# Three narrow router products: from stationary activations to stationary weights on three column groups, issued in steps

## The chip, the cores and the metric

The kernel runs on one core of a Trainium2 chip. The metric is the device time in microseconds of one execution. It was run three times; the median is the number to be changed. One further execution was recorded by the hardware profiler, and all times "by the profile" are from that one, counted from the start of its span.

## The reference

The reference is one forward pass of a graph network on 512 tokens of 768 features, in four blocks. Each block adds a graph layer and an attention layer to x, and then a feed-forward layer. The feed-forward layers of blocks 0, 2 and 3 are mixtures of experts; each begins with a router, which is a product of the normalized tokens with a very narrow matrix. Cut to the routers (in the case's names):

```python
# block 0: 8 experts of 192, two per token, weights from sqrt(softplus)
scores  = jnp.sqrt(jax.nn.softplus(flat @ gate_w))            # [512,768] @ [768,8]
_, indices = jax.lax.top_k(scores + gate_bias, 2)
weights = take_along_axis(scores, indices, axis=1); weights /= clip(weights.sum(1), 1e-06)
# block 2: a shared expert and 3 routed ones, two per token
routing_probs = jax.nn.sigmoid(x @ router_w + routing_bias)   # [512,768] @ [768,3]
scores, indices = jax.lax.top_k(routing_probs, 2); scores /= scores.sum(-1)
# block 3: 8 experts, one per token, at most 64 tokens each
router_probs = jax.nn.softmax(xf @ router_w)                  # [512,768] @ [768,8]
expert_gate, expert_index = max(router_probs), argmax(router_probs)
```

All is in float32.

## The kernel before

Tokens lie token-major, as 4 tiles of 128 tokens (`NT`), or feature-major, as 6 chunks of 128 features by 512 tokens (`KC`; `xfT` is the normalized input of a feed-forward layer in this form). `normed` makes both: layernorm on VectorE (DVE), transposes on TensorE (PE, L246), copies out of PSUM in turn by ScalarE (ACT, L202) and DVE (L204). It returns the second half of the transposes as a function `rest`, which the next product calls after its first four parts.

Nearly all large products are one level of Strassen's scheme. `strassen_feature` (products at L461, feature-major result) works in three chunks of seven products, each of three 128x256 matmuls; `strassen_add` (L553) adds its results into x. The sums of the left operand are made by DVE (L392 to L394), those of the weights by GpSimd (POOL, `SplitB`, L411 to L414) ahead of time from weights that the SP queue has loaded. `staged` delays the second half of each chunk behind the first half of the next one, also across calls. A float32 matmul stands in the profile as two records, each with its own weight load ("PEld"); they are called passes here. So the 24 matmuls of a router are 48 passes.

After each of these products the kernel calls `tick`, which takes one step of the first generator in the list `background`; side work is so put between products of the main stream. `delayed(9, step)` waits nine ticks and then does all of its step at once. The written order is only the start: instructions of different streams are then placed on each engine by a scheduler, and the order on each engine is fixed before the run; each engine works through its own in order.

`router` (L338) loads the narrow weights `rt_w` (768 by `e`, with `e` 8 or 3) and, for each token tile, runs six matmuls in which the 128x128 piece of `xfT` is stationary and the `e` columns of the weights are moving (L345). Its result is [token, expert] in PSUM. It is used in three places:

- Block 0, `weights_by_expert`: ten ticks into the first `strassen_feature` of `up_part(0)`, the router and all that follows run in one piece: copy of the logits to `lg` (L954), softplus by Abs, Exp and Ln on ACT with small DVE operations between, Sqrt, `ranks` (a comparison of all pairs of experts, L330 to L335), normalization, four transposes of the weights `sc` (L985), a copy and a write to DRAM (`c_dram`, L988), from which `load_weights` reads rows spread over partitions into `pc` (L1000). `pc` multiplies the hidden values in `multiplied` (L1019, POOL).
- Block 2, `route`: called between the first two `strassen_feature` of the shared expert; logits plus bias in `pr` (L1565), Sigmoid, `ranks`, normalization. It is first used by the down product of the first routed expert.
- Block 3: right after `normed`, with no other product beside it; the maximum of the logits (L1656), Exp, `ranks`, positions by small matmuls (L1676), and then dispatch, experts and output. This is the end of the kernel.

`row_tile` gives row buffers from a pool of two, which the bias rows (`row`, L168) use as well; `psum` gives one of eight PSUM banks.

Of the kernel before, what the change touches and what calls it, by code (L numbers as in the profile page):

```python
# [97 lines left out]
def kernel(ctx: ExitStack, tc: tile.TileContext, a: dict, out: bass.AP):  # L98
# [27 lines left out]
    def psum():  # L126
        return psp.tile([P, 512], FP, tag="ps", name="ps")
# [35 lines left out]
    def row_tile(name, n=D):  # L163
        return rowp.tile([P, KC * (P + 2)], FP, tag="row", name=name)[:, :n]
# [170 lines left out]
        V.tensor_reduce(r, gt, AX.X, ALU.add)  # L335
        return r

    def router(xT, w_dram, e):  # L338

        w = small.tile([P, KC, e], FP, tag="rt_w", name="rt_w", bufs=2)  # L340
        nc.sync.dma_start(w, w_dram.rearrange("(k p) e -> p k e", p=P))
        ps = psum()[:, : NT * e].rearrange("p (t e) -> p t e", t=NT)
        for t in range(NT):
            for k in range(KC):
                T.matmul(ps[:, t, :], xT[:, k, ts(t, P)], w[:, k, :], start=k == 0, stop=k == KC - 1)  # L345
        return ps

# [75 lines left out]
    def drain():  # L425
        while background:
            tick()

    def delayed(n, step):

        for _ in range(n):
            yield
        step()

    held = []

# [510 lines left out]
    _, xfT, xs, rest = normed(x, "xf", 1e-5)  # L947
    with tc.tile_pool(name="ffn0", bufs=2) as fp:
        E = 8
        def weights_by_expert():  # L950
            gb = tiny(E, name="gb")
            nc.sync.dma_start(gb, spread(a["L0_ffn_gate_bias"], 0, E))
            lg = tiny(NT, E, name="lg")
            V.tensor_copy(lg, router(xfT, a["L0_ffn_gate_w"], E))  # L954

            ex, u, big, sm = (tiny(NT, E, name=n) for n in ("sp_e", "sp_u", "sp_b", "sp_s"))
            S.activation(ex, lg, AF.Abs)
            S.activation(ex, ex, AF.Exp, scale=-1.0)
            V.tensor_scalar(u, ex, 1.0, None, op0=ALU.add)
            S.activation(big, u, AF.Ln)  # L960
            V.tensor_scalar(sm, ex, -1.0 / 3.0, 0.5, op0=ALU.mult, op1=ALU.add)
            V.tensor_mul(sm, sm, ex)
            V.tensor_scalar(sm, sm, -1.0, 1.0, op0=ALU.mult, op1=ALU.add)
            V.tensor_mul(sm, sm, ex)
            V.tensor_scalar(u, ex, 0.01, None, op0=ALU.is_lt)
            V.tensor_sub(sm, sm, big)
            V.tensor_mul(sm, sm, u)
            V.tensor_add(big, big, sm)
            V.tensor_scalar(lg, lg, 0.0, None, op0=ALU.max)
            V.tensor_add(lg, lg, big)  # L970
            sc = tiny(NT, E, name="sc")
            S.activation(sc, lg, AF.Sqrt)
            V.tensor_add(lg, sc, gb[:, None, :].to_broadcast([P, NT, E]))
            sel = ranks(lg, E)
            V.tensor_scalar(sel, sel, 2.0, None, op0=ALU.is_lt)
            V.tensor_mul(sc, sc, sel)
            tot = tiny(NT, name="tot")
            V.tensor_reduce(tot, sc, AX.X, ALU.add)
            V.tensor_scalar(tot, tot, 1e-6, None, op0=ALU.max)
            V.reciprocal(tot, tot)  # L980
            for t in range(NT):
                V.tensor_scalar(sc[:, t, :], sc[:, t, :], tot[:, t : t + 1], None, op0=ALU.mult)
            ps = psum()
            for t in range(NT):
                T.transpose(ps[:E, ts(t, P)], sc[:, t, :], ident)  # L985
            scT = row_tile("scT", N)[:E]
            V.tensor_copy(scT, ps[:E])
            nc.sync.dma_start(c_dram, scT)  # L988


        c_dram = tc.dram_tile([E, N], FP, name="c_dram")
        pc = fp.tile([P, KC, N], FP, name="pc", bufs=1)

        def load_weights(g):
            for f in range(KC):
                p = 0
                while p < P:
                    at = g * D + f * P + p
                    n = min(P - p, 192 - at % 192)
                    nc.sync.dma_start(pc[p : p + n, f, :],  # L1000
                                      c_dram[at // 192 : at // 192 + 1, :].to_broadcast([n, N]))
                    p += n

        def up_part(g):

            hid = feature_major("hid")
            sums = SplitA(hid, G, False)

            def gated(c, i, j, ps):
                h = hid[:, 3 * j + c, ts(i, HT)]  # L1010
                V.tensor_scalar(h, ps, 10.0, None, op0=ALU.min)
                S.activation(h, h, AF.Silu)

            def multiplied(c, i, j, ps):
                f = 3 * j + c
                h = hid[:, f, ts(i, HT)]
                V.tensor_scalar(ps, ps, -10.0, 10.0, op0=ALU.max, op1=ALU.min)
                V.tensor_mul(h, h, ps)
                G.tensor_mul(h, h, pc[:, f, ts(i, HT)])  # L1019

            if g == 0:
                background.append(delayed(9, weights_by_expert))
            strassen_feature(xs, ready(a["L0_ffn_w1"][:, ts(g, D)]) if g else nexts.pop(), gated, None,
                             None if g else rest)
            yield
            load_weights(g)
            strassen_feature(xs, ready(a["L0_ffn_w3"][:, ts(g, D)]), multiplied,
                             sums.sums)
            flush()
            yield sums  # L1030

        pending = None
        for g in range(2):
            stages = up_part(g)
            next(stages)
            if pending:
                strassen_add(pending[1], ready(a["L0_ffn_w2"][ts(pending[0], D), :]), add_part)
            pending = g, next(stages)

        sw = w_tile()  # L1040
        wi = sw[:, : KC * 384].rearrange("p (k n) -> p k n", k=KC)
        for i, n in enumerate(("w1s", "w3s")):
            src = a[f"L0_ffn_{n}"].rearrange("(k p) n -> p k n", p=P)
            nc.sync.dma_start(wi[:, :, ts(i, P)], src[:, :, :P])
            nc.sync.dma_start(wi[:, :, 2 * P + i * HD : 2 * P + (i + 1) * HD], src[:, :, P:])
        w2a, w2b = sw[:, KC * 384 : KC * 384 + D], sw[:HD, KC * 384 + D : KC * 384 + 2 * D]
        nc.sync.dma_start(w2a, a["L0_ffn_w2s"][:P, :])
        nc.sync.dma_start(w2b, a["L0_ffn_w2s"][P:, :])
        last = ready(a["L0_ffn_w2"][D:, :])
        gat_w1 = ready(a["L1_gnn_W1"])  # L1050
        hid = feature_major("hid")

        def glu(dst, pg, pu):
            V.tensor_scalar(dst, pg, 10.0, None, op0=ALU.min)
            S.activation(dst, dst, AF.Silu)
            V.tensor_scalar(pu, pu, -10.0, 10.0, op0=ALU.max, op1=ALU.min)
            V.tensor_mul(dst, dst, pu)

        pg, pu = feature_product(wi, xfT, 0), feature_product(wi, xfT, P)
        glu(hid[:, 0, :], pg, pu)  # L1060
        ps = feature_product(wi, xfT, 2 * P)
        glu(hid[:HD, 1, :], ps[:HD], ps[HD:])
        strassen_add(pending[1], last, add_part)
        flush()
        token_product([hid[:, 0, :], hid[:HD, 1, :]], lambda k: (w2a, w2b)[k], add_to_x)
# [492 lines left out]
    with tc.tile_pool(name="ffn2", bufs=2) as fp:  # L1558
        E = 3
        pr = tiny(NT, E, name="pr")  # L1560

        def route():
            rb = tiny(E, name="rb")
            nc.sync.dma_start(rb, spread(a["L2_ffn_routing_bias"], 0, E))
            V.tensor_add(pr, router(xfT, a["L2_ffn_router_w"], E), rb[:, None, :].to_broadcast([P, NT, E]))  # L1565
            S.activation(pr, pr, AF.Sigmoid)
            sel = ranks(pr, E)
            V.tensor_scalar(sel, sel, 2.0, None, op0=ALU.is_lt)
            V.tensor_mul(pr, pr, sel)
            tot = tiny(NT, name="tot")  # L1570
            V.tensor_reduce(tot, pr, AX.X, ALU.add)
            V.reciprocal(tot, tot)
            V.tensor_mul(pr, pr, tot[:, :, None].to_broadcast([P, NT, E]))
# [43 lines left out]
        for e in range(E + 1):  # L1617
            for g in range(2):
                stages = up_part(e, g)
                next(stages)  # L1620
                if pending:
                    down_part(*pending)
                else:
                    route()
                pending = e, g, next(stages)
        down_part(*pending)
        flush()
# [23 lines left out]
    with tc.tile_pool(name="ffn3", bufs=1) as fp:  # L1651
        E, CAP = 8, N // 8
        lg = tiny(NT, E, name="lg")
        mx = tiny(NT, name="mx")
        ps = router(xfT, a["L3_ffn_router_w"], E)
        V.tensor_reduce(mx, ps, AX.X, ALU.max)  # L1656
        V.tensor_sub(lg, ps, mx[:, :, None].to_broadcast([P, NT, E]))
        S.activation(lg, lg, AF.Exp)
        V.tensor_reduce(mx, lg, AX.X, ALU.add)
        V.reciprocal(mx, mx)  # L1660
# [169 lines left out]
```

## Time and profile before

| what | value |
|---|---|
| median of 3 runs (lowest to highest) | 3228.47 us (3226.35 to 3235.73) |
| the profiled execution: its time, its span | 3229.27 us, 3227.6 us |
| PE, weight loads, DVE, ACT, POOL: busy share | 96%, 64%, 47%, 20%, 45% |
| mean granted TensorE clock | 0.981 |
| chain that ended last: PE, DVE, POOL | 81%, 9%, 4% |
| matmuls of the Strassen products on that chain (L461, L553) | 39%, 22% |
| router matmuls (L345) | 144 passes, median 256 ns each, overlapping |

A record of a matmul covers its own latency as well, and the next one starts before it ends; so the distance between starts is what a pass costs, and it is read from stretches: 12 passes of 128x256 in 2.75 us. "PEclk" is the clock that TensorE was granted, 1.00 at full speed. A bracket at the end of a line is idle time of the engine just before it, and what ended it. A busy PE need not be a fast one: the clock has to be read beside it.

### The profile page before, as it was taken

How to read it: one execution, taken by the hardware profiler on the slowest of the kernel's cores; microseconds unless marked ns; L12 is line 12 of the kernel's file. 1: busy time of each engine (PE TensorE's matmuls, PEld its weight loads, DVE VectorE, ACT ScalarE, POOL GpSimd, SP SyncE). 2: the span in 40 equal slices, each digit the busy share in tenths (PEclk: the TensorE clock that was granted, in tenths of full speed). 3: DMA queues.
4: the chain of work that ended last, by engine and by line, in shares of the span. 5: the costliest groups of instructions: out<-in, count | busy, mean ns of one | idle time of the engine just before them, and what ended most of it. 6: DMA issues, size and time to landing. Idle time of an engine off the chain costs nothing.

```text
span 3227.6 us, 32219 instructions
## 1 busy us (share of the span) xinstructions
PE 3094.6 (96%) x12097; PEld 2066.8 (64%) x12097; DVE 1524.1 (47%) x3433; ACT 637.7 (20%) x1268; POOL 1461.4 (45%) x1560
## 2 busy tenths in 40 slices
PE   8999999999999999999998999999999999999999
PEld 3445555555765776765684357777777775677755
DVE  7574444445446324446676535433333336453241
ACT  0132222222252110201441212100000001121101
POOL 0344444445225564464534254355555557355520
PEclk9999999999999999999999999999999999999999
DMA  3021221112202122321111422122222222131221
GB/s 111 14 79 69 69 69 69 69 69 108 88 30 93 59 101 76 108 94 68 45 67 68 119 82 98 59 88 88 89 88 88 89 86 84 70 108 59 89 97 59
DMA packets 92837, 255.23 MB, mean 79 GB/s; under 512 B 9905, under 2 KB 14897, under 8 KB 91530
## 3 DMA queue, kind: packets, MB, share of 16 engines
q1 hardware_dynamic: 92682, 253.18, 22.7%
q8 instruction: 95, 1.56, 0.2%
q14 instruction: 60, 0.49, 0.0%
HBM read 244.23 MB, written 8.93 MB: 78 GB/s over the span
## 4 chain that ended last, share of the span: by engine, by line
PE 81%; DVE 9%; POOL 4%; issue 3%; ACT 1%; DMA 0%; SPq 0%; POOLq 0%; DVEq 0%; ACTq 0%
PE ps L461 39%; PE ps L553 22%; PE ps L751 4%; PE ps L614 3%; PE ps L302 3%; DVE st_u L664 2%; PE ps L922 1%; PE ps L909 1%; PE ps L246 1%; DVE edge_w L637 1%; DVE edge_w L639 1%; POOL tw L411 1%; POOL w L412 1%; POOL tw L413 1%; PE ps L1711 1%
## 5 line engine op out<-in xcount | busy, mean ns | idle before, releaser
L411 POOL TENSOR_TENSOR tw<-w 128x384 f32<-128x384 f32 x246 | 249.9, 1025 | 1094.0 <-PE ps L461 324.0
L461 PE MATMUL ps<-sx,tw 128*128 128x256 f32 x1188 | 304.8, 381 | 3.3 <-DVE sx L393 2.3
L461 PE MATMUL ps<-sx,w 128*128 128x256 f32 x1188 | 293.2, 383 | 0.8 <-DVE room L1264 0.8
L553 PE MATMUL ps<-tw,sx 128*128 128x384 f32 x720 | 252.3, 489 | 9.6 <-POOL tw L413 5.8
L412 POOL TENSOR_TENSOR w<-w 128x384 f32<-128x384 f32 x246 | 253.0, 1036 | 8.5
L413 POOL TENSOR_TENSOR tw<-w 128x384 f32<-128x384 f32 x246 | 252.4, 1033 | 9.5
L414 POOL TENSOR_TENSOR tw<-w,tw 128x384 f32<-128x384 f32 x246 | 250.3, 1024 | 9.9
L553 PE MATMUL ps<-w,sx 128*128 128x384 f32 x720 | 252.5, 486 | 0.0
L461 PEld LDWEIGHTS ps<-sx,w 128*128 128x128 f32 x1188 | 227.4, 192 | 34.5 <-DVE room L1264 1.5
L461 PEld LDWEIGHTS ps<-sx,tw 128*128 128x128 f32 x1188 | 226.4, 191 | 35.4 <-PE ps L461 3.4
L553 PEld LDWEIGHTS ps<-tw,sx 128*128 128x128 f32 x720 | 136.1, 190 | 106.5 <-POOL sx L383 8.0
L583 DVE TENSOR_TENSOR x<-x,ps 128x384 f32<-128x384 f32 x218 | 116.1, 552 | 185.9 <-PE ps L553 185.7
L553 PEld LDWEIGHTS ps<-w,sx 128*128 128x128 f32 x720 | 136.8, 190 | 92.8
L504 DVE TENSOR_TENSOR st_u<-st_p,ps 128x256 f32<-128x256 f32 (+1 forms) x127 | 57.1, 450 | 271.9 <-PE ps L461 271.9
L477 ACT COPY st_p<-ps 128x256 f32<-128x256 f32 (+1 forms) x127 | 50.2, 395 | 667.5 <-PE ps L461 665.6
L461 PE MATMUL ps<-xfT,w 128*128 128x256 f32 x720 | 180.2, 389 | 0.1
L461 PE MATMUL ps<-tw,sx 128*128 128x384 f32 x456 | 166.7, 499 | 14.0 <-DVE st_u L499 6.0
L751 PE MATMUL ps<-edge_wT,h 128*128 128x512 f32 x384 | 168.0, 594 | 8.7 <-DVE edge_wT L204 8.7
L499 DVE TENSOR_TENSOR st_u<-st_p,ps 128x256 f32<-128x256 f32 (+1 forms) x127 | 57.1, 450 | 246.8 <-PE ps L461 143.0
L461 PE MATMUL ps<-w,sx 128*128 128x384 f32 x456 | 160.5, 489 | 1.0 <-DVE ps L505 1.0
L461 PEld LDWEIGHTS ps<-xfT,w 128*128 128x128 f32 x720 | 140.2, 195 | 24.2 <-ACT st_p L477 0.3
L553 PE MATMUL ps<-w,hid 128*128 128x384 f32 x432 | 143.1, 487 | 0.0
(460 smaller groups left out, 5093.3 us busy)
## 6 DMA issues: line engine op xcount, KB each, us to landing
w<-in_L_gnn_W SPq DMA_DIRECT2D x60, 768.0 KB, 6.2
w<-in_L_mix_fc_w SPq DMA_DIRECT2D x48, 768.0 KB, 6.9
row<-in_rows SPq DMA_DIRECT2D x39, 384.0 KB, 3.6
w<-in_L_mix_qkv_w SPq DMA_DIRECT2D x18, 768.0 KB, 7.3
w<-in_L_ffn_w SPq DMA_DIRECT2D x18, 768.0 KB, 6.7
w<-in_L_ffn_routed_gate SPq DMA_DIRECT2D x18, 768.0 KB, 6.0
w<-in_L_ffn_routed_up SPq DMA_DIRECT2D x18, 768.0 KB, 5.9
w<-in_L_ffn_routed_down SPq DMA_DIRECT2D x18, 768.0 KB, 6.0
```

The costliest lines, as they stand in the source:

```text
L302: T.matmul(ps, parts[k][:, ts(t, P)], w_of(k)[:, ts(c, HC)], start=k == 0, stop=k == n - 1)
L411: G.tensor_sub(tt[:, 0, k], b22[:, k], b12[:, k])
L412: G.tensor_sub(b12[:, k], b12[:, k], b11[:, k])
L413: G.tensor_sub(tt[:, 1, k], b22[:, k], b12[:, k])
L414: G.tensor_sub(tt[:, 2, k], b21[:, k], tt[:, 1, k])
L461: T.matmul(bank, l, r, start=start and k == 0, stop=stop and k == KC // 2 - 1, skip_group_check=True)
L499: V.tensor_add(b["u2"], b["p1r"], b["y"])
L553: T.matmul(b[name], l[:, k, ts(m, P)], r[:, k, :], start=start and k == 0, stop=k == KC // 2 - 1, skip_group_check=True)
L583: V.tensor_add(x[:, t, ts(j, HC)], x[:, t, ts(j, HC)], ps)
L614: T.matmul(acc[t], oh[:, 1, ts(t, P)], oh[:, 0, :], start=j == 0, stop=j == EC - 1)
L664: V.scalar_tensor_tensor(junk, h[:, t, :], 1.0, r, op0=ALU.mult, op1=ALU.mult, accum_out=sc[:, t : t + 1])
L751: T.matmul(ps, h[:, s, ts(f, P)], wT[:, s, :], start=s == 0, stop=s == NT - 1)
```

## The change

The router's operands change roles. The weights are padded with zeros to 32 columns per feature chunk (`rt_w` is now [128, 6, 32], one buffer, cleared by POOL and then loaded) and are stationary; `xfT` is moving, 512 tokens at a time. Three feature chunks go to three column groups of 32, which write partitions 0 to 31, 32 to 63 and 64 to 95 of one PSUM bank; two rounds of three add up all six chunks. The 96x512 result is copied to SBUF by ACT, and four small matmuls, with 128 tokens of it stationary and a constant `three` (three unit matrices below each other) moving, turn it to [token, expert] and add the three groups. The function is a generator, with steps between the product, the small matmuls and what follows. In block 0 it now starts at the fifth tick instead of the tenth and its chain is cut into pieces by `yield`; `drain()` finishes it before `load_weights`. In block 2 `route` is put into `background` too, and runs beside the second `strassen_feature`. In block 3 it is run through at once.

```diff
-    def router(xT, w_dram, e):
-        w = small.tile([P, KC, e], FP, tag="rt_w", name="rt_w", bufs=2)
-        nc.sync.dma_start(w, w_dram.rearrange("(k p) e -> p k e", p=P))
+    G3 = 3 * 32
+    three = const.tile([P, 8], FP, name="three")
+    V.tensor_add(three, ident[:, 0:8], ident[:, 32:40])
+    V.tensor_add(three, three, ident[:, 64:72])
+    def router_weights(w_dram, e):
+        w = small.tile([P, KC, 32], FP, tag="rt_w", name="rt_w", bufs=1)
+        G.memset(w, 0.0)
+        nc.sync.dma_start(w[:, :, :e], w_dram.rearrange("(k p) e -> p k e", p=P))
+        return w
+    def routed(w, xT, e, use):
+        ps = psum()
+        for r in range(KC // 3):
+            for g in range(3):
+                k = 3 * r + g
+                T.matmul(ps[ts(g, 32)], w[:, k, :], xT[:, k, :], start=r == 0, stop=r == KC // 3 - 1,
+                         skip_group_check=True)
+        part = row_tile("rt_p", N)
+        S.copy(part[:G3], ps[:G3])
+        yield
+        yield
         ps = psum()[:, : NT * e].rearrange("p (t e) -> p t e", t=NT)
         for t in range(NT):
-            for k in range(KC):
-                T.matmul(ps[:, t, :], xT[:, k, ts(t, P)], w[:, k, :], start=k == 0, stop=k == KC - 1)
-        return ps
+            T.matmul(ps[:, t, :], part[:G3, ts(t, P)], three[:G3, :e], start=True, stop=True)
+        use(ps)
...
-    def delayed(n, step):
+    def delayed(n, steps):
         for _ in range(n):
             yield
-        step()
+        yield from steps
...
+        rw = router_weights(a["L0_ffn_gate_w"], E)
         def weights_by_expert():
...
-            V.tensor_copy(lg, router(xfT, a["L0_ffn_gate_w"], E))
+            yield from routed(rw, xfT, E, lambda ps: V.tensor_copy(lg, ps))
             S.activation(ex, lg, AF.Abs)
             S.activation(ex, ex, AF.Exp, scale=-1.0)
+            yield
...
             V.tensor_scalar(u, ex, 0.01, None, op0=ALU.is_lt)
+            yield
...
             S.activation(sc, lg, AF.Sqrt)
+            yield
+            yield
...
+            for _ in range(4):
+                yield
             ps = psum()
             for t in range(NT):
                 T.transpose(ps[:E, ts(t, P)], sc[:, t, :], ident)
...
-                background.append(delayed(9, weights_by_expert))
+                background.append(delayed(4, weights_by_expert()))
...
             yield
+            if g == 0:
+                drain()
             load_weights(g)
...
         def route():
-            V.tensor_add(pr, router(xfT, a["L2_ffn_router_w"], E), rb[:, None, :].to_broadcast([P, NT, E]))
+            yield from routed(rw, xfT, E, lambda ps: V.tensor_add(
+                pr, ps, rb[:, None, :].to_broadcast([P, NT, E])))
             S.activation(pr, pr, AF.Sigmoid)
+            yield
+            yield
...
-                    route()
+                    background.append(route())
...
-        ps = router(xfT, a["L3_ffn_router_w"], E)
-        V.tensor_reduce(mx, ps, AX.X, ALU.max)
-        V.tensor_sub(lg, ps, mx[:, :, None].to_broadcast([P, NT, E]))
+        def scores(ps):
+            V.tensor_reduce(mx, ps, AX.X, ALU.max)
+            V.tensor_sub(lg, ps, mx[:, :, None].to_broadcast([P, NT, E]))
+        for _ in routed(router_weights(a["L3_ffn_router_w"], E), xfT, E, scores):
+            pass
```

On the engines, the order differs from before only around the three places. In block 0, PE now has: two matmuls of the product A22·T4, the first router matmul, one more of A22·T4, the other five router matmuls, three of A22·T4 for the next chunk, three on `sx`, the four small matmuls; the four transposes of `sc` follow 27 matmuls later (the first of them one matmul ahead of the other three). In block 2, the six router matmuls stand together after the first product of the second `strassen_feature`, and the small ones six matmuls later. In block 3, they follow the 24 transposes of `normed`.

## The prediction

> **What bounds the kernel now.** The page first: PE is 96% busy and holds 81% of the chain that ended last, so a saving counts only where PE works for nothing, works slowly, or waits. Then the timeline around the three router places, the granted clock by stretches, and the rows of narrow matmuls elsewhere. Block 0 and block 2:
>
> ```profile
> 1281.43 2.75 PE L461 MATMUL ps<-sx,tw 128*128 128x256 f32 x12
> 1284.02 7.40 PE L345 MATMUL ps<-rt_w,xfT 128*128 128x8 f32 x48
> 1291.27 2.05 PE L461 MATMUL ps<-sx,w 128*128 128x256 f32 x4
> 1293.12 2.77 PE L461 MATMUL ps<-sx,tw 128*128 128x256 f32 x6
> 1303.76 1.02 PE L985 MATMUL ps<-ident,sc 128*8 128x128 f32 x4 [7.02 <-DVE sc L982]
> ...
> 2068.47 6.84 PE L345 MATMUL ps<-rt_w,xfT 128*128 128x3 f32 x48
> 2075.18 2.91 PE L461 MATMUL ps<-xfT,w 128*128 128x256 f32 x6
> ```
>
> A Strassen pass costs (2.75 - 0.17)/12 = 0.215 us, a router pass 7.40/48 = 0.154 or 6.84/48 = 0.143. After the router, six passes take 2.8 to 2.9 instead of 1.46, and PE then waits 7.02 for the weights' chain. The clock, for block 0, 2 and 3 (columns: stretch, its length, PE busy, clock, DMA share, GB/s):
>
> ```profile
> 1283.80:1291.20 7.40, 7.40 (x50) 0.73 0.01 2
> 1291.20:1308.50 17.30, 10.28 (x30) 0.62 0.15 31
> 1308.50:1330.00 21.50, 21.50 (x101) 1.00 0.62 181
> 2068.20:2075.20 7.00, 7.00 (x52) 0.79 0.00 0
> 2075.20:2079.70 4.50, 4.50 (x13) 0.57 0.00 0
> 2079.70:2100.00 20.30, 20.30 (x95) 1.00 0.32 117
> ```
>
> So a router costs its own passes and the clock of the passes behind it. Block 3 stands alone; its end hangs on the last copy of `xfT` and the router:
>
> ```profile
> 3124.75 2.21 DVE L204 COPY xfT<-ps 128x256 f32<-128x256 f32 x6
> 3125.70 5.61 PE L345 MATMUL ps<-rt_w,xfT 128*128 128x8 f32 x46
> 3131.35 0.19 DVE L1656 TENSOR_REDUCE mx<-ps 128x4 f32<-128x32 f32 x1 [4.39 <-PE ps L345]
> ```
>
> Last, what is known of parts of the array:
>
> ```profile
> 898.12 2.74 PE L896 MATMUL ps<-qkT,wf 64*128 64x512 f32 x12
> 3182.02 0.86 PE L1742 MATMUL ps<-w,hid 64*64 64x384 f32 x2
> 3182.81 0.86 PE L1740 MATMUL ps<-w,hid 128*64 128x384 f32 x2
> 3183.60 0.86 PE L1742 MATMUL ps<-w,hid 64*64 64x384 f32 x4
> 895.00:992.00 97.00, 97.00 (x534) 62.31 (x531) 50.30 (x73) 54.85 (x101) 22.28 (x22) 1.00 0.06 23
> ```
>
> A pass of 512 columns costs 512 x 0.215/256 = 0.43. L896 alternates two row halves: 12 passes in 2.74 is six times 0.43 plus 0.16, so the halves run side by side. Of L1742, four passes last as long as two; in the written order they are the second half of one bank's partitions and the first half of the next one's, two column groups. So column groups overlap in float32 too. Where L1742 and L1740 alternate, the starts are 0.79 apart for two passes of 0.32: a change of array shape costs 0.79 - 0.64 = 0.15. Half arrays (stretch 895 to 992) held the clock at 1.00.
>
> **The change, part by part.**
>
> *The wide products.* Per router 12 passes of 0.43: 5.16 if serial, 1.72 if three groups overlap, plus two shape changes (0.30). In block 0 one product stands alone ahead of the others (0.86 for its two passes), and the five others pack into 1.72: 2.58, with four shape changes 0.60, in all 3.2. I take overlap. Three groups writing one bank have no row here (L1742's two go to different banks). The Trainium skill (TensorE: Matmul & The Clock Gate, Measured speedup vs the span model) gives three column tiles 2.38 times, not 3: 5.16/2.38 = 2.17 instead of 1.72, an estimate, +0.45 in blocks 2 and 3 and less in block 0, +1.2 in all. I keep the row's full overlap and carry the 1.2 in the range.
>
> *The small products.* Eight passes each, bound by weight loads: 5.61/46 = 0.122 at nearly full clock, so 1.0.
>
> A rule that speaks against the whole change: the skill (TensorEngine Tiling (Array Packing), Instruction Overhead) has a matmul with one moving column last as long as one with 60. Taken alone, that makes the old passes about 0.025 at its 2.4 GHz: 48 cost 1.2, the new form of block 2 with eight small ones 1.72 + 0.30 + 0.2 = 2.2, and the change would lose 1.0 or more per router, some 4 in all. The rows say 0.12 to 0.15, because a full 128x128 weight load goes with every pass; the row decides. The same page says that a mode change drains the array; the rows price that at 0.15.
>
> *Block 0.* From the first router weight load (1283.80) to the first products at full rate (1308.45) 24.65 pass. Needed: 24 Strassen passes, 5.16, and the four turns of `sc`, 0.6. Excess 18.9: the router, the halved clock, the wait of 7.02. After: 3.2 + 1.0, less the 0.65 that PE waited at 1278.76 for `sx`, which the router now fills. It comes in at about 1276; `xfT` is complete at 1276.14, so it waits some 0.1. The chain from `lg` to `sc` took 12.3 (1291.45 to 1303.7), among it four ACT table loads of 1.28. In the new order 18 evacuations instead of six stand between its DVE operations; 12 more at about 0.35, partly in gaps of the chain, make it about 15. PE has 27 matmuls = 54 passes = 11.6 between the small products and the first turn. So PE waits about 3 there; bounds 0 and 5. DVE's waits for the table loads (L982, L990, L999) stand ahead of evacuations, but each ends before PE has made the next bank that they hold. Cost after 3.2 + 1.0 - 0.65 + 3 = 6.5; saved 12.4. If that wait drops the clock for some 7 us at half, 3.4 less.
>
> *Block 2.* 2068.26 to 2079.53 is 11.27 for 12 passes, 2.58: excess 8.7. After: 1.72 + 0.30 + 1.0 = 3.0. The copy of the result (0.59 by the 128x512 copies at L202) has six passes twice, 2.6, as cover. Table loads are as before; `ranks` moves among evacuations and is due much later. Saved 5.7.
>
> *Block 3.* From the last `xfT` copy (3126.96) to the first DVE read (3131.35) 4.39. After: the last group's two passes, 0.86 + 0.4 queued behind the round before, latency 0.17; copy 0.59 and about 0.25 of hand-over; eight small passes, 1.0 + 0.17. About 3.4. Saved 1.0; nothing covers this place, so serial groups show in full.
>
> *At nothing.* The two additions for `three` (about 0.2 each) fall into DVE's start; from 26 us on DVE waits for PE in the one-hot loop, so at most 0.4, and I add 0.2. With one `rt_w` buffer, POOL clears it after the last router: behind the clearing stand L1019 (first at 1320) and L411 at 2086.47, which POOL awaited for 36 us. The loads of `rt_w` behind the clearings hold SP until about 1280 and 2071; next in SP are a bias row wanted later and weights issued at 1323 and 2085. If the products behind gain 13 and 6, some 30 and 8 are still left. `rt_p` takes one row buffer between rows long used.
>
> Sum 12.4 + 5.7 + 1.0 - 0.2 = 18.9 from 3229.27 gives 3210.4. That execution lies 0.8 above the median, so 3209.6; 3210.
>
> **The rivals.**
>
> *A: no overlap in three groups of one bank* (15%). Block 0 costs 2.6 more, block 2 3.4 and block 3 3.0: 18.9 - 9.0 = 9.9 saved, 3218.6. For: no row has three groups in one bank. Against: L1742 and L896.
>
> *B: the weights' chain stays exposed in block 0* (13%). PE waits 7 as before, and the clock halves for about 7 us: 7.4 less saved, 11.5 in all, 3217. For: in-order DVE and ACT with four table loads between evacuations. Against: its start moves 8 us earlier and 54 passes stand beside it.
>
> *C: slower, through the clock* (4%). If the gate took 32 working columns of 128 for an idle array, passes would be serial and at half clock, 0.86 instead of 0.43. Saving A is used up when each of the 36 passes costs 0.28 more, at 0.71 per pass; at 0.86 it is 15.5 - 9.9 = 5.6 slower, 3234. Against: half arrays ran at 1.00 for 97 us.
>
> *D: not what it says* (3%): later stages catch on another wait and give all but a few microseconds back, 3226. Against: PE's order elsewhere is untouched, and it is the chain.
>
> **How the numbers follow.** My forecast has 65%: its own range is 3205 (no wait at the turns, block 3 with more overlap) to 3215 (wait 5, the skill's 2.38). A and B stretch the range to 3219. With 3204 at the bottom, for a clock that stays full in block 3 as well, it leaves out about 2 in 10. About 0.3% (9.7 us) is what a measurement of this kernel can tell from no change: faster is below 3218.8. The forecast lies below it, and so do most of B and half of A: 65 + 12 + 8 = 85%. Same takes the rest of A and B and most of D, 11%; slower is C, 4%.
>
> **What would show it right or wrong.** The router rows become 12 passes of 32x512 lasting about 2 (3 with the one alone in block 0), not 5.3; clock 1.00 in the stretches behind them; products behind the router at 1.46 for six passes; the wait in front of the turns below 5; the first DVE read in block 3 about 3.4 after the last `xfT` copy. Wrong: passes 0.43 apart (A), a wait of 7 (B), clock near 0.5 during the wide passes (C).

## The result, and the profile after

The changed kernel takes 3209.29 us (median of four runs, 3209.14 to 3209.59) against 3228.64 us (3226.35 to 3235.73) on the same chip: ratio 0.9936, 95% interval 0.9919 to 0.9954. In a later comparison it took 3210.39 us (3208.71 to 3211.21) against 3230.34: 0.9941, 0.9928 to 0.9953. The forecast was 3210. The profiled execution took 3209.59 us, span 3207.8, clock 0.984.

PE's timeline around the routers of block 0 and block 2 (columns: start, length, engine and line, operation, tiles, shapes, count; L357 is the wide product, L365 the small one, L1013 the turns of `sc`):

```profile
1277.65 1.04 PE L357 MATMUL ps<-xfT,rt_w 128*32 128x512 f32 x2
...
1279.26 1.91 PE L357 MATMUL ps<-xfT,rt_w 128*32 128x512 f32 x10
1281.10 1.56 PE L481 MATMUL ps<-xfT,tw 128*128 128x256 f32 x6
...
1283.79 0.96 PE L365 MATMUL ps<-three,rt_p 96*128 96x8 f32 x8
1284.61 1.54 PE L481 MATMUL ps<-sx,w 128*128 128x256 f32 x6
...
1298.38 0.27 PE L1013 MATMUL ps<-ident,sc 128*8 128x128 f32 x1 [1.85 <-DVE sc L1008]
...
2056.09 1.46 PE L481 MATMUL ps<-xfT,w 128*128 128x256 f32 x6
2057.47 1.92 PE L357 MATMUL ps<-xfT,rt_w 128*32 128x512 f32 x12
2059.32 1.56 PE L481 MATMUL ps<-xfT,w 128*128 128x256 f32 x6
...
2062.02 0.95 PE L365 MATMUL ps<-three,rt_p 96*128 96x3 f32 x8
2062.83 1.54 PE L481 MATMUL ps<-sx,w 128*128 128x256 f32 x6
```

Twelve wide passes last 1.92: four rounds of 0.43 and the latency of the last, so three groups run as one. Behind the router six Strassen passes take 1.54 to 1.56 where they took 2.8 to 2.9, and the wait at the turns is 1.85 instead of 7.02. The clock beside and behind block 0's router and beside block 2's (columns: stretch, its length, busy time of PE, its weight loads, DVE, ACT and POOL, granted clock, DMA share, GB/s):

```profile
1276.60:1285.00 8.40, 8.40 (x40) 4.93 (x41) 5.37 (x9) 1.01 (x3) 1.81 (x4) 1.00 0.05 1
1285.00:1298.30 13.30, 11.53 (x54) 9.70 (x52) 9.74 (x41) 10.62 (x17) 0.00 (x0) 1.00 0.09 32
2057.40:2063.00 5.60, 5.60 (x34) 3.77 (x34) 0.84 (x2) 2.24 (x3) 0.26 (x1) 1.00 0.07 4
```

It is full beside the router, behind it and through the wait. Block 3, from the last copy of `xfT` to the first DVE read of the scores:

```profile
3106.59 2.08 DVE L204 COPY xfT<-ps 128x256 f32<-128x256 f32 x6
3107.45 2.46 PE L357 MATMUL ps<-xfT,rt_w 128*32 128x512 f32 x12
3109.95 0.58 ACT L360 COPY rt_p<-ps 96x512 f32<-96x512 f32 x1 [2.00 <-PE ps L357]
3110.58 1.06 PE L365 MATMUL ps<-three,rt_p 96*128 96x8 f32 x8 [0.67 <-ACT rt_p L360]
3111.68 0.19 DVE L1692 TENSOR_REDUCE mx<-ps 128x4 f32<-128x32 f32 x1 [3.00 <-PE ps L365]
```

From 3108.67, where the last copy ends, to 3111.68 are 3.01 us; it was 4.39. Of the chain that ended last, PE now holds 82%, DVE 9% and POOL 4%: nothing has taken PE's place.

To say where the 19.8 us of span came from, three stretches are measured in every kernel, each between two events that belong to the same work. Block 0: from the first pass of A22·T4 (`xfT,tw`, 128x256) to DVE's first clip of a result of the second product. Block 2: from the issue of the first load of the shared gate's weights to that of the first load of the shared down's. Block 3: from the first load of `w2a` to the first of `w2b`. The first of them in both kernels, by stretch; before:

```profile
1275.24:1318.80 43.56, 35.88 (x159) 30.70 (x160) 18.84 (x57) 11.72 (x21) 1.57 (x3) 0.80 0.23 56
```

and after:

```profile
1276.58:1306.36 29.78, 27.93 (x131) 21.63 (x132) 17.84 (x57) 12.34 (x22) 1.83 (x4) 1.00 0.16 42
```

PE's idle time falls from 7.68 to 1.85, its busy time from 35.88 to 27.93, and the mean clock rises from 0.80 to 1.00. Block 0 saves 43.56 - 29.78 = 13.78, block 2 115.85 - 110.14 = 5.71, block 3 54.24 - 52.98 = 1.26. That is 20.75. Against it stand 1.3 at the start (below), and 0.4 in favour lie elsewhere: 19.8. Between the blocks the two traces keep the same distance: 1.34 us late at block 0, 12.45 early at block 2's first load after 13.78 were saved.

### The profile page after: what moved, and what is told of

It is laid out like the page before. It is cut to its first block, busy times and chain, and to the rows that moved or that the text cites. A ratio compares the mean times of both kernels' runs of the same rounds, so it can differ in the third digit from the quotient of the medians.

```text
span 3207.8 us, 32057 instructions
## 1 busy us (share of the span) xinstructions
PE 3079.4 (96%) x12003; PEld 2047.6 (64%) x12013; DVE 1525.1 (48%) x3435; ACT 639.4 (20%) x1271; POOL 1460.8 (46%) x1563
## 3 DMA queue, kind: packets, MB, share of 16 engines
q8 instruction: 94, 1.54, 0.2%
## 4 chain that ended last, share of the span: by engine, by line
PE 82%; DVE 9%; POOL 4%; issue 3%; ACT 1%; DMA 0%; SPq 0%; POOLq 0%; DVEq 0%; ACTq 0%
PE ps L481 39%; PE ps L573 22%; PE ps L771 4%; PE ps L634 3%; PE ps L302 3%; DVE st_u L684 2%; PE ps L942 1%; PE ps L929 1%; PE ps L246 1%; DVE edge_w L657 1%; POOL tw L431 1%; POOL w L432 1%; PE ps L1750 1%; POOL tw L433 1%; DVE edge_w L659 1%
```

## The experiments

All in one table; the blocks' stretches are those just defined, from one profiled execution each.

| kernel | median us (range) | ratio to before, 95% | block 0 | block 2 | block 3 |
|---|---|---|---|---|---|
| before | 3228.64, 3230.37 and 3230.34 in three comparisons | | 43.56 | 115.85 | 54.24 |
| changed | 3209.29 (3209.14 to 3209.59) | 0.9936, 0.9919 to 0.9954 | 29.78 | 110.14 | 52.98 |
| `e1_one_group` | 3219.89 (3217.44 to 3221.33) | 0.9971, 0.9959 to 0.9983 | 32.60 | 112.20 | 56.73 |
| `e2_steps_only` | 3222.84 (3218.19 to 3225.73) | 0.9977, 0.9967 to 0.9986 | 33.41 | 115.84 | 54.24 |
| `e3_groups_only` | 3220.39 (3217.39 to 3221.98) | 0.9974, 0.9962 to 0.9985 | 40.26 | 110.09 | 52.93 |
| `e4_later` | 3207.21 (3204.89 to 3208.76) | 0.9932, 0.9919 to 0.9944 | 27.44 | 110.09 | 52.97 |
| `r_after` | 3210.39 (3208.71 to 3211.21) | 0.9941, 0.9928 to 0.9953 | 29.77 | 110.16 | 52.99 |
| `e5_best` | 3206.37 (3204.67 to 3207.01) | 0.9927, 0.9914 to 0.9941 | 27.43 | 108.49 | 53.55 |
| `e6_narrow_spread` | 3216.41 (3215.78 to 3220.29) | 0.9963, 0.9949 to 0.9976 | 30.10 | 110.95 | 54.24 |

`e1` to `e4` ran on one chip, `r_after`, `e5` and `e6` on another. The theory under test: the old router cost its own narrow passes, a halved clock behind them, and in block 0 a wait for the weights' chain; the column groups take away the first two, the steps the third. The rivals: three groups in one bank do not overlap, or the steps alone explain the gain. "The steps" are two things, the earlier start and the cutting into pieces; no run has one without the other. "At half" is a granted clock of 0.50; it comes in steps of about 3.4 us, as the section on the hardware shows.

### One column group instead of three

```diff
-        for r in range(KC // 3):
-            for g in range(3):
-                k = 3 * r + g
-                T.matmul(ps[ts(g, 32)], w[:, k, :], xT[:, k, :], start=r == 0, stop=r == KC // 3 - 1, ...)
+        for k in range(KC):
+            T.matmul(ps[:32], w[:, k, :], xT[:, k, :], start=k == 0, stop=k == KC - 1)
...
-            T.matmul(ps[:, t, :], part[:G3, ts(t, P)], three[:G3, :e], start=True, stop=True)
+            T.matmul(ps[:, t, :], part[:32, ts(t, P)], three[:32, :e], start=True, stop=True)
```

> The changed kernel with all six wide products on one column group (partitions 0 to 31) instead of three, so that nothing can run side by side; the small products then add nothing up, they only turn. Theory (the three groups run fully side by side): the 12 passes of a router go from 4 times 0.43 (block 0: 6 times) to 12 times 0.43, which is 2.6 more in block 0, 3.4 in block 2, 3.0 in block 3, plus about 0.3 per router for the small products' own array shape (32 rows): about 3218 to 3219, nearly half of the gain gone. Rival (it is the steps that bring the gain, the groups matter little): within 2 us of the changed kernel, 3209 to 3211.

Its timeline, block 0 and block 2:

```profile
1278.37 4.48 PE L355 MATMUL ps<-xfT,rt_w 128*32 128x512 f32 x10
...
2058.34 5.34 PE L355 MATMUL ps<-xfT,rt_w 128*32 128x512 f32 x12
```

and its clock in the router of block 0:

```profile
1276.60:1287.00 10.40, 10.40 (x38) 5.04 (x37) 4.63 (x7) 0.69 (x2) 0.92 (x2) 1.00 0.04 1
```

The same passes in one group last 5.34 instead of 1.92. With the latency of 0.17 taken off both, (5.34 - 0.17)/(1.92 - 0.17) = 2.95. So the overlap of three is whole to within 2%. Without it block 0 is 2.82 us longer, block 2 2.06 and block 3 3.75. The last two differ from the 3.4 and 3.0 expected by the clock: it stood at half one step less in block 2's layernorm (18 passes there take 4.76 instead of 6.40), and one more in block 3. This kernel is rival A made real, and its 3219.89 stands where A's 3218.6 was put. It answers rival C as well: with 32 of 128 columns at work and no overlap, the clock is 1.00.

### The steps alone

The product as before (`xfT` stationary, 48 narrow passes in one run), in the new places and steps:

```diff
-        for r in range(KC // 3):
-            for g in range(3):
-                ...
-        S.copy(part[:G3], ps[:G3])
         yield
         yield
...
         for t in range(NT):
-            T.matmul(ps[:, t, :], part[:G3, ts(t, P)], three[:G3, :e], start=True, stop=True)
+            for k in range(KC):
+                T.matmul(ps[:, t, :], xT[:, k, ts(t, P)], w[:, k, :e], start=k == 0, stop=k == KC - 1)
```

> The changed kernel's steps, start at the fifth tick and place in the background list, but with the old product (24 matmuls with 8 or 3 moving columns each). Theory (narrow passes cost their weight loads, and the clock behind them): block 0 keeps the hidden chain, but its router takes 6 to 7.4 again instead of 4.2 and the clock falls to half for about 7 us behind it, 5 to 6 lost; block 2 loses 5.7 and block 3 1.5: about 3222. Rival (the clock fell because PE waited for the weights' chain, not because of the narrow passes): clock 1.00 behind the router in block 0, about 3218, and block 2 below the loss of 5.7.

PE's timeline:

```profile
1280.76 5.42 PE L358 MATMUL ps<-rt_w,xfT 128*128 128x8 f32 x48
1286.03 2.56 PE L474 MATMUL ps<-sx,w 128*128 128x256 f32 x6
...
1301.15 0.27 PE L1006 MATMUL ps<-ident,sc 128*8 128x128 f32 x1 [1.16 <-DVE sc L1001]
...
2064.77 7.24 PE L358 MATMUL ps<-rt_w,xfT 128*128 128x3 f32 x48
2071.88 2.91 PE L474 MATMUL ps<-sx,w 128*128 128x256 f32 x6
```

The timeline shows the 48 passes in one run and slow products behind. The clock behind block 0's router, then in block 2's and behind it:

```profile
1286.10:1302.00 15.90, 14.64 (x61) 11.88 (x61) 10.39 (x43) 10.30 (x17) 0.26 (x1) 0.89 0.10 26
2064.70:2071.90 7.20, 7.20 (x51) 7.17 (x49) 0.69 (x2) 0.00 (x0) 0.00 (x0) 0.73 0.00 0
2071.90:2078.00 6.10, 6.10 (x23) 5.16 (x24) 2.83 (x14) 1.50 (x2) 0.26 (x1) 0.76 0.08 7
```

Block 2 is what it was, to 0.01 us: a step there hides nothing, since PE is the bound and its passes are the same. In block 0 PE waits 1.16 at the turns instead of 7.02, and 10.15 us are saved. It loses 3.6 to the changed kernel there, not the 5 to 6 expected: behind the narrow passes the clock was at half for one step, 0.11 x 15.9 x 2 = 3.5 us, not two; the work done in it takes some 1.7 us longer. The rest is the dearer product, and a wait of 0.81 for `sx`, which the changed kernel's router fills. In block 2's two stretches PE is busy without a gap, 7.20 of 7.20 and 6.10 of 6.10, and still the clock falls.

### The groups alone

```diff
-                background.append(delayed(4, weights_by_expert()))
+                def at_once():
+                    for _ in weights_by_expert():
+                        pass
+                    yield
+                background.append(delayed(9, at_once()))
...
-                    background.append(route())
+                    for _ in route():
+                        pass
```

> The changed kernel's product on three groups, but in block 0 in one piece at the tenth tick as before, and in block 2 in one piece between the two products. Theory (in block 0 the larger part is the hidden chain): PE waits about 10 for the turns, since the chain of about 12 has only 8 passes beside it, and the clock falls behind that wait; block 0 loses 8 to 11 of its 13.8, block 2 at most 0.5, block 3 nothing: 3217 to 3220. Rival (the product's shape and the clock are the gain, the chain would be hidden anyway): within 3 us, 3209 to 3212.

PE's timeline in block 0, and then the clock from the router to the turns:

```profile
1285.75 1.92 PE L357 MATMUL ps<-xfT,rt_w 128*32 128x512 f32 x12
...
1301.88 1.01 PE L1013 MATMUL ps<-ident,sc 128*8 128x128 f32 x4 [10.53 <-DVE sc L1008]
```

```profile
1285.70:1301.80 16.10, 5.65 (x33) 3.49 (x32) 7.97 (x33) 10.78 (x15) 0.26 (x1) 0.82 0.10 27
```

The router is short, PE reaches the turns sooner and waits longer for the same chain: 10.53 instead of 7.02. In block 0 the groups alone save 3.30, in blocks 2 and 3 all that the change saves there; the median, 3220.39, lies 0.4 above the range expected. The steps' 10.15 and the groups' 3.30 are 13.45, and both together gave 13.78, so in block 0 the parts add up to within 0.33. The clock falls here without a narrow pass, in the wait. It had done so in the kernel before as well, where the wait of 7.02 ended at 1303.76:

```profile
1300.20:1306.80 6.60, 3.04 (x10) 2.37 (x11) 4.24 (x15) 1.48 (x2) 0.00 (x0) 0.54 0.01 2
```

So the theory is too simple in one point: in block 0 the halved clock was not the narrow passes' alone. It stood at half for about 17 us of that stretch before (0.20 x 43.56 x 2), for 3.5 with the steps alone and for about 10 with the groups alone (0.18 x 16.1 x 2 up to the turns, 0.12 x 18.2 x 2 in the 18.2 us behind). The steps, which take away the wait, take away its clock too.

### The turns later

The turns of `sc` wait three ticks longer, and the router starts one tick later:

```diff
-            for _ in range(4):
+            for _ in range(7):
                 yield
...
-                background.append(delayed(4, weights_by_expert()))
+                background.append(delayed(5, weights_by_expert()))
```

> The changed kernel with the router of block 0 one tick later (sixth instead of fifth) and its four turns three ticks later. Theory (what is left to gain in block 0 is the product that stands alone, 0.86, two changes of array shape, 0.3, and PE's wait of 1.9 for the turns): 2 to 3 less, 3206 to 3207.5. Rival (the turns wait for a DVE that is full with evacuations, or PE meets the wait elsewhere): 3208.5 to 3209.5.

PE's timeline in block 0:

```profile
1279.40 1.92 PE L357 MATMUL ps<-xfT,rt_w 128*32 128x512 f32 x12
...
1289.48 1.56 PE L481 MATMUL ps<-sx,tw 128*128 128x256 f32 x6 [0.60 <-DVE st_u L519]
...
1299.94 0.60 PE L1013 MATMUL ps<-ident,sc 128*8 128x128 f32 x4
```

The wait of 1.85 at the turns is gone, but PE now waits 0.60 at 1289.48 for an evacuation on DVE (`st_u`), which it did not before: the rival has a part of it. Block 0 takes 2.34 less. PE's idle time gives 1.25 of that (1.85 to 0.60), its busy time 1.09 (27.93 to 26.84, at a clock of 1.00 in both): the wide passes now stand in one row, without a product alone and with one pair of shape changes less.

### The changed kernel again, and a version to beat it

`r_after` is the changed kernel, unaltered, as a partner. `e5_best` is `e4_later` and, in block 3 alone, the copy of the partial scores shared by two engines (shown in short: a flag that only block 3 sets chooses the new form):

```diff
-        S.copy(part[:G3], ps[:G3])
+        S.copy(part[:G3, :HT], ps[:G3, :HT])
+        V.tensor_copy(part[:G3, HT:], ps[:G3, HT:])
```

> The changed kernel unaltered, so that the next kernel has its partner on the same chip. Expected 3209 to 3210 us again. With the 3207.2 us of the kernel that takes the turns three ticks later, the difference of those two is so far one between two calls; this run makes it one within a call.

> The changed kernel with two alterations: in block 0 the turns of the scores wait three ticks longer (as in e4_later, which removed the 1.85 us wait of TensorE there), and in block 3, where the small products wait for the whole copy of the partial scores out of PSUM (a copy of 512 columns on ScalarE, 0.58 us in block 0), one half of that copy goes to VectorE. Theory: the copy in block 3 is on the path to the softmax and half of it takes about 0.3 us less, block 0 gives 2.3: the total is 2.3 to 2.7 us below the changed kernel. Rival: VectorE starts its half late or the fixed part of each half is most of its time; block 3 is unchanged and the total is 2.0 to 2.3 below. Rival of the first alteration: what e4_later gained was the difference between two calls; then the total is within 1 us of the changed kernel.

The timeline of `e5_best` in block 3:

```profile
3106.59 0.37 ACT L361 COPY rt_p<-ps 96x256 f32<-96x256 f32 x1 [1.99 <-PE ps L357]
3106.99 0.42 DVE L362 COPY rt_p<-ps 96x256 f32<-96x256 f32 x1 [1.68 <-ACT rt_p L361]
3107.01 1.07 PE L369 MATMUL ps<-three,rt_p 96*128 96x8 f32 x8 [0.46 <-ACT rt_p L361]
3108.12 0.19 DVE L1696 TENSOR_REDUCE mx<-ps 128x4 f32<-128x32 f32 x1 [0.70 <-PE ps L369]
```

All five runs of `e5_best` (at most 3207.01) lie below all five of `r_after` (at least 3208.71): it beats both kernels. In block 0 it repeats `e4_later` (27.43). The second alteration is hardly shown. The halves do not run side by side: DVE starts 0.40 later, and the bracket says that it was ACT's write of the same tile that released it. Still the small products start on the first half, and the scores are read 2.80 after the last copy of `xfT` instead of 3.01: 0.2 gained. The whole of block 3 is 0.56 longer, though: in this execution the clock was at half for one step more behind it, and the 48 passes of 512 columns that follow (from 3118.93) took 22.70 us, where they took 21.93 in `r_after`. The stretches with their clock, `r_after`, then `e5_best`:

```profile
3108.00:3115.00 7.00, 2.92 (x20) 1.59 (x16) 3.46 (x13) 2.09 (x3) 0.00 (x0) 0.97 0.61 141
3115.00:3125.00 10.00, 7.84 (x28) 6.36 (x29) 5.16 (x18) 0.00 (x0) 0.00 (x0) 0.51 0.01 2
```

```profile
3108.00:3115.00 7.00, 3.00 (x15) 2.95 (x15) 3.25 (x12) 0.49 (x2) 0.00 (x0) 0.58 0.04 12
3115.00:3125.00 10.00, 8.44 (x21) 4.94 (x22) 5.64 (x17) 0.45 (x1) 0.00 (x0) 0.61 0.01 2
```

Twice the missing clock times the length, over both stretches, is 10.2 us at half in the one and 13.7 in the other. Between the two medians lie 4.0 us, where 2.3 to 2.7 were expected; only 2.34 of them, block 0's, can be put down to the edit. The spans of the two profiled executions differ by 2.7. Beside block 0's 2.34, places that the edit does not touch give 1.7 (block 2's layernorm, with one step fewer at half) and 0.7 (an earlier start); block 3 takes 0.56 back, and 1.5 go between the blocks and at the end. `e4_later` and `e5_best` cannot be told apart by their ratios.

### The narrow product, spread out

As `e2_steps_only`, with a step after each token tile, so that wide products come between the narrow passes. The edit also drops the two steps that `e2_steps_only` has ahead of the product, so the narrow passes start two ticks earlier:

```diff
-        yield
-        yield
...
         for t in range(NT):
             for k in range(KC):
                 T.matmul(ps[:, t, :], xT[:, k, ts(t, P)], w[:, k, :e], start=k == 0, stop=k == KC - 1)
+            if t < NT - 1:
+                yield
```

> The narrow product of the kernel before, 48 passes with 8 columns (3 in block 2), cut by token tile: 6 passes a tick with a wide Strassen product between them, and everything else as in e2_steps_only, where the 48 passes stood in one run (5.42 us in block 0, 7.24 us in block 2, and the granted clock low after them). It separates the price of a narrow pass from the price of what the clock does after a long run of them. Theory: each pass keeps its 0.11 to 0.12 us, and with at most some 0.7 us of narrow passes in a piece the clock stays full; block 2 then keeps 48 x 0.107 = 5.1 us and loses 3 us against the kernel before (about 112.8 us from its first load to its last), block 0 loses about 11.5 of its 43.6 us, block 3 stays at 54.2, and the total is 3217 to 3218. Rival: narrow passes lower the clock however they are spread; block 2 stays near 115.8, block 0 near 33.4, and the total is near the 3222 of e2_steps_only.

PE's timeline in block 2, and then the clock in the routers of block 0 and block 2:

```profile
2058.64 2.74 PE L356 MATMUL ps<-rt_w,xfT 128*128 128x3 f32 x24
...
2063.91 1.40 PE L356 MATMUL ps<-rt_w,xfT 128*128 128x3 f32 x12
2065.17 1.54 PE L474 MATMUL ps<-sx,w 128*128 128x256 f32 x6
```

```profile
1277.00:1287.00 10.00, 10.00 (x71) 9.43 (x71) 4.54 (x7) 0.00 (x0) 0.79 (x2) 1.00 0.01 2
2058.60:2068.00 9.40, 9.40 (x68) 8.91 (x68) 0.86 (x3) 1.66 (x2) 0.00 (x0) 1.00 0.00 0
```

The scheduler made pieces of up to 2.96 us out of it, longer than intended, and still the clock is 1.00 in both routers. A pass costs (2065.17 - 2063.91)/12 = 0.105 us, where it cost 0.143 in one run of 48. Block 2 saves 4.90; 1.55 of that is its layernorm, where 18 passes took 4.79 instead of 6.34, and 3.35 is the router's, for 3 in the theory. Block 0 saves 13.46, nearly as much as in the changed kernel, which waited 1.85 at the turns where this one has only the 0.60 at `st_u` of `e4_later`. The median, 3216.41, is 0.6 below the range expected. The total falls short of the blocks' sum: the span shrinks by 13.5 for 18.4. Against before, the trace loses 0.8 at the start, 3.1 between block 0 and block 2 and 1.0 behind block 2. Of the 3.1, 1.6 go where the mean clock over the same 25 us of work (from 1585 in before) is 0.80 against 0.86; the other losses were not followed up.

So the clock behind the old router was the price of a *run* of narrow passes. Block 2 shows it, where no wait is in play; in block 0 the earlier start helps as well. Spreading them takes that away without any packing. Packing is then worth, against `e4_later` in block 0 (both at a full clock, both with the wait of 0.60), 30.10 - 27.44 = 2.7 us, and in block 2, with the layernorm's 6.40 - 4.79 = 1.61 put back, (110.95 + 1.61) - 110.14 = 2.4. In block 3, where neither is spread and the clock is at half behind both, it is 1.3. Together that is about 6.4 of the 20.8. The clock and the wait were the larger part.

## Why the prediction was right

*Three groups overlap.* Shown by the 1.92 against 5.34. In block 2 the next product starts 1.94 later than without the router (2059.32, less 2056.09 and six passes of 0.216), for 2.02 in the sum. The Trainium skill (TensorE: Matmul & The Clock Gate, Measured speedup vs the span model) has 2.38 for three column tiles; here it is 2.95, in float32 and in one bank, and the measurement decides. The 1.2 kept in the range for it were not needed.

*The rule against the change* (the Trainium skill, TensorEngine Tiling (Array Packing), Instruction Overhead, that one column costs as much as 60) was rightly put behind the rows: even at a full clock a narrow pass is 0.105 us, and `e2_steps_only` and `e6_narrow_spread` show block 2 at 5.7 and, with the layernorm evened out, 2.4 us more with the old product, where the rule would have had the change lose 1.0 or more per router.

*The small products*: 0.82 and 0.81, for 1.0. The term came from narrow passes of 0.122 "at nearly full clock"; at a full clock a pass of these is 0.10.

*Block 0*: predicted 12.4, measured 13.8. 1276.58 to 1281.10 is 4.52, of which six passes of A22·T4 are 1.29: the wide products cost 3.23, for 3.2. The mis-sized term is the wait at the turns, 3 against 1.85. PE's side was right (54 passes in 11.8, for 11.6); the chain was not. It took 13.5 us from the copy of `lg` at 1284.79 to `sc` at 1298.3, for "about 15": 16 evacuations stand on DVE in it, not 18, so ten were added and not twelve, and they made it 1.2 longer than the 12.3 of before, which is less than the 2.7 allowed for. At 1.85 the wait left the clock at 1.00, so the 3.4 us named for that case did not fall due. The bounds 0 and 5 held, and `e4_later` shows the lower one.

*Block 2*: predicted 5.7, measured 5.71. *Block 3*: predicted 3.4 from copy to read, measured 3.01; small amounts in three places: 1.28 for 1.43 until the copy starts, 0.63 for 0.84 of copy and hand-over, 1.10 for 1.17 of small products. The stretch shrank by 1.26, for 1.0.

*The total* came within 1 us of the forecast, and in part by luck. In the profiled execution the three blocks gave 20.75, for 19.1 in the sum, and a late start, which the change did not make (below), took 1.3 back.

*At nothing, and 0.2 for `three`.* The clearing of `rt_w` and its loads delayed nothing, as said: the distance between the traces doesn't move there. The one-hot loop starts 1.2 us later in the profiled execution (11.19 for 9.98). In the timeline before it:

```profile
8.48 1.02 DVE L221 BATCH_NORM_STATS2 ln_st<-x 128x6 f32<-128x384 f32 x2 [2.40 <-DMA x<-in_x]
```

The two additions for `three` take 0.15 and 0.16 us. The tile of `x` that DVE waited for here was begun at 8.48, and at 7.37 before. In the other executions with `three` the loop began at 9.68 to 10.47, and at 9.98 before; so it is when a transfer lands, and not the change.

*The rivals.* A is refuted by the 1.92; `e1_one_group`, where it holds, loses 8.6 in the three blocks, for the 9.0 put on it. B came only in part: a wait of 1.85 in the changed kernel, and 10.53 without the steps. C is refuted by the clock of 1.00 in one group and in three. D: the later stages gave nothing back. The range's lower end, a full clock in block 3, did not come: there the clock was at half for 10.2 us after, 13.7 before.

## What to carry to other kernels

Read the clock beside every stretch of narrow matmuls: here a run of them cost its passes once and slowed the next products for some 3 to 10 us, and breaking up the run gave back most of that before any packing was done. Where no wide products are at hand to spread it among, or on top of that, a narrow product can be turned round so that the wide operand moves, with the narrow one on several column groups; three groups took a third of the time of one. When a chain of small operations hangs on such a product, start it early and put the wait for its end behind enough other work: 54 passes were too few for a chain of 13.5 us, and with 66, three ticks later, the wait was gone.

## What the runs showed of the hardware

The clock can fall while PE is busy without a gap. In `e2_steps_only` 48 narrow passes fill 7.20 us with matmuls and weight loads, and the clock is 0.73 in it; with wide products between, the same passes leave it at 1.00 (`e6_narrow_spread`). Passes of 512 columns on 32 columns of the array left it at 1.00 (`e1_one_group`). So it is not enough that instructions are issued; that it depends on how much moves through the array would fit, but no run varied that alone.

In these traces the clock has two levels, 1.00 and 0.50, and goes from one to the other in steps of about 3.4 us. The Trainium skill (TensorE: Matmul & The Clock Gate, What's actually happening) describes both, a free-running window of 3413 ns; the stretches below agree (3.2 to 3.6 us at half in one, at least 6.70 in the other), and show what it does to a comparison. Block 2's layernorm, work that no edit touched, in the changed kernel (the timeline, then the stretch with its clock):

```profile
2027.82 6.40 PE L481 MATMUL ps<-xfT,w 128*128 128x256 f32 x18
```

```profile
2025.80:2032.50 6.70, 6.02 (x17) 5.04 (x18) 3.09 (x6) 2.77 (x5) 3.59 (x4) 0.50 0.53 207
```

and in `e5_best`:

```profile
2025.74 4.74 PE L485 MATMUL ps<-xfT,w 128*128 128x256 f32 x18
```

```profile
2020.00:2023.60 3.60, 0.87 (x6) 0.64 (x6) 3.60 (x16) 0.40 (x2) 3.60 (x4) 1.00 0.95 358
2023.80:2027.00 3.20, 2.60 (x9) 2.34 (x10) 3.01 (x5) 1.12 (x3) 2.96 (x4) 0.50 1.02 404
2027.20:2030.60 3.40, 3.40 (x19) 2.96 (x18) 0.00 (x0) 2.12 (x4) 0.35 (x1) 1.00 0.03 7
```

Two steps at half against one: the same 18 passes take 6.40 or 4.74 us. So this place alone can move an execution by 1.7 us, which is as much as several of the terms here. So a single edit is judged by its own stretch and the clock in it, and not by the total alone.
